# One GpSimd drain more behind the first scatter of the last pair of output tiles: sparse attention over a graph

## The chip, the cores and the metric

The kernel runs on one core of a Trainium2 chip. The metric is the device time of one execution in microseconds (us). The kernel before takes 637.19 us, the median of three runs (636.75 to 637.22).

The core's engines run side by side, each with its own stream of instructions: TensorE (PE; PEld are its weight loads), VectorE (DVE), ScalarE (ACT), GpSimd (POOL) and SyncE (SP). They wait for each other by semaphores. An engine's own sequencer takes its instructions in order; waits, branches and drains are the sequencer's work (in the profile POOLq, SPq and so on).

## The reference

A pre-norm layer with attention over a sparse graph: 2708 nodes of 1024 features, and a 0/1 matrix `adj` with a share of 0.0014771 ones, some four in a row.

```python
h = jnp.maximum(_layernorm(x, axis=-1), 0.0)
q = h @ W_q.T + b_q
k = h @ W_k.T + b_k
v = h @ W_v.T + b_v
z = scale * (q @ k.T)
spare_z = z * adj
spare_z = jnp.where(spare_z == 0.0, -10000.0, spare_z)
attn = jax.nn.softmax(spare_z, axis=1)
return x + jax.nn.relu(attn @ v)
```

## The kernel before

The kernel never forms the 2708 x 2708 scores. It finds each row's few neighbours in `adj`, and sorts the rows by their number of neighbours, so that the 21 full tiles of 128 sorted rows (and a rest of 20) each need about the same number of gathers. `ptab` holds, for each sorted place, the neighbours' row numbers and the row's own number (column `SLOTS`).

The stages, in order:

- M = W_q^T W_k is formed on TensorE from the weights as they come in; meanwhile rows of x are normed to h and stored to HBM, and VectorE searches `adj`.
- Ten "q" units: each takes two tiles of h and multiplies them with M. A unit is a two by two block product with seven multiplications instead of eight (`multiply`), two tiles of 128 rows against a 1024 x 1024 matrix.
- Beside them, for each tile, GpSimd gathers the neighbours' rows of h, VectorE takes their products with q, ScalarE the exponentials, and VectorE the weighted sum u of the gathered rows (`scores`, `weights`, `sums`).
- Ten "o" units: the same block product of two tiles of u with W_v. The tiles' order is fixed by the list `order`; its last entry is tile 8, which is left over and handled alone at the end.

An output tile is brought back to its place by an indirect DMA of GpSimd (`scatter`): the rows of y go to the rows of `out` whose numbers stand in `ptab`. All GpSimd DMAs, gathers and scatters, direct and indirect, go through one queue whose descriptors GpSimd makes itself.

The last o unit is the pair of tiles 16 and 9. For it `o_results` returns what `ends` returns: the rows of x are gathered ahead into ya (tile 16) and yb (tile 9), and as each bank of the product is done, VectorE adds the halves (`joined_x`: max with 0, plus x). `multiply` calls the four results in the order `c11` (left half of ya), `c12` (right half of ya), `c22` (right half of yb), `c21` (left half of yb). So tile 16 is complete in `c12`, which ends with its scatter, and tile 9 only in `c21`, after two more block products. Between them TensorE also starts the single tile 8.

Tile 8 follows with three block products; its right half is joined on VectorE and scattered (`scatter_half`), then the left half. Ahead of them, a flag is formed that tells whether the fast path held for this input; every engine reads it, and the branch behind it skips a general version of the kernel (lines 1390 on) that these inputs don't need. At the end (the profile gives it line 1562) SyncE waits for the landing of every DMA and for the other engines, and a barrier over all engines follows: each engine's sequencer drains and signals, GpSimd collects the signals and releases the others. These drains are put there by the framework; the kernel's own text has none.

The stream of GpSimd is not written out by hand at this point: a scheduler places instructions by their dependences, and `tc.issue_after(i)` places what is written under it behind instruction i on the same engine, without a wait for i to end.

Of the kernel before, what the change touches and what calls it, by code (L numbers as in the profile page):

```python
# [65 lines left out]
def tile_preln_masked_attention(  # L66
# [12 lines left out]
    nc = tc.nc  # L79
# [527 lines left out]
    def gather(dst, src, t, w, n, skip=False):  # L607
        off = bass.IndirectOffsetOnAxis(ap=ptab.bitcast(U32)[:n, t, w:w + 1], axis=0)
        if skip:
            return nc.gpsimd.indirect_dma_start(out=dst, out_offset=None, in_=src, in_offset=off,  # L610
                                                bounds_check=N - 1, oob_is_err=False)
        return nc.gpsimd.indirect_dma_start(out=dst, out_offset=None, in_=src, in_offset=off)
# [192 lines left out]
    outs = []  # L805

    def scatter(y, t, n):
        to = nc.gpsimd.indirect_dma_start(  # L808
            out=out, out_offset=bass.IndirectOffsetOnAxis(ap=ptab.bitcast(U32)[:n, t, SLOTS:SLOTS + 1], axis=0),
            in_=y[:n], in_offset=None)  # L810
        for other in outs:
            tc.declare_no_dep(to.ins, other.ins, reason="rows of a permutation")
        outs.append(to)
# [297 lines left out]
    def o_results(ta, tb):  # L1111
        ya = work.tile([P, D], FT, tag="q", name=f"y_{ta}", bufs=4)
        yb = work.tile([P, D], FT, tag="q", name=f"y_{tb}", bufs=4)
        if (ta, tb) == o_pairs[-1]:
            return ends(ya, ta, yb, tb)

        def c11(X):
            nc.scalar.activation(ya[:, lo], X, AF.Relu)

        def c22(Y, p5):  # L1120
            nc.vector.tensor_add(p5, copied(Y), p5)
            nc.scalar.activation(yb[:, hi], p5, AF.Relu)

        def c12(Z, u2):
            nc.vector.tensor_add(u2, Z, u2)
            nc.scalar.activation(ya[:, hi], u2, AF.Relu)  # L1126
            if ta == NT - 2:

                nc.sync.dma_start(tail_dram, ya[P - 1:, :])
            due.append((now[0], 5, ya, ta))  # L1130

        def c21(Y):
            nc.scalar.activation(yb[:, lo], Y, AF.Relu)
            due.append((now[0] + 1, 1, yb, tb))

        return c11, c22, c12, c21

    def ends(ya, ta, yb, tb):

        send(gather(ya, x, ta, SLOTS, P))  # L1140
        gather(yb, x, tb, SLOTS, P)

        def joined_x(y, cols, a):
            nc.vector.scalar_tensor_tensor(y[:, cols], a, 0.0, y[:, cols], op0=ALU.max, op1=ALU.add)

        def c11(X):
            joined_x(ya, lo, X)

        def c22(Y, p5):
            nc.vector.tensor_add(p5, Y, p5)  # L1150
            joined_x(yb, hi, p5)

        def c12(Z, u2):
            nc.vector.tensor_add(u2, Z, u2)
            joined_x(ya, hi, u2)
            scatter(ya, ta, P)

        def c21(Y):
            joined_x(yb, lo, Y)
            scatter(yb, tb, P)  # L1160

        return c11, c22, c12, c21
# [10 lines left out]
    def send(behind, stay=0):  # L1173

        while len(sent) > stay:
            with tc.issue_after(behind.ins):
                scatter(*sent.pop(0))
# [388 lines left out]
```

## Time and profile before

| what | value |
| --- | --- |
| median of three runs | 637.19 us (636.75 to 637.22) |
| span of the profiled execution, first to last instruction | 635.2 us |
| busy: TensorE, its weight loads | 624.2 us, 316.4 us |
| busy: VectorE, GpSimd, ScalarE | 523.9, 367.3, 285.9 us |
| GpSimd's DMA queue | 27,088 packets, 86.02 MB |
| mean granted clock of TensorE | 0.996 |
| issue to landing of the last pair's and the last tile's scatters (five from 600 us on) | 2.7 to 5.3 us |

The profile is of one execution; its span leaves out what lies before the first and after the last instruction, and so is some 2 us under the median. Busy time counts work alone: waits, branches and drains of a sequencer are not in it, and where they matter they have to be asked for by their line. In rows of the profile, "x3: 46/109/7122, 627.2 to 634.9" means three instructions with the shortest, median and longest duration in ns, and the start of the first and the last in us.

### The profile page before, as it was taken

The page shows a single profiled execution, that of the slowest core. Times are in us where ns is not written, and L with a number is a line of the kernel's source. Part 1 is how long each engine was busy: PE and PEld are TensorE (multiplying, and loading weights), DVE is VectorE, ACT ScalarE, POOL GpSimd, SP SyncE. Part 2 cuts the span into 40 slices and gives each one's busy share as a digit, 9 for nine tenths or more (in the row PEclk, how much of TensorE's full clock was granted, in tenths as well). Part 3 has the DMA queues.
Part 4 walks back from the last instruction along what each step waited for, and adds up shares of the span by engine and source line. Part 5 has one row for each costly group of instructions (what it writes and reads, how often), then busy time and mean ns, then how long its engine had stood idle before and what let it go on. Part 6 is the DMA issues. An engine that isn't in the chain of part 4 may idle for free.

```text
span 635.2 us, 6138 instructions
## 1 busy us (share of the span) xinstructions
PE 624.2 (98%) x1627; PEld 316.4 (50%) x1627; DVE 523.9 (82%) x1020; ACT 285.9 (45%) x423; POOL 367.3 (58%) x397
## 2 busy tenths in 40 slices
PE   9999999999999999999999999999999999999993
PEld 5777766444444544444444444444444444444441
DVE  5999888998896755997889999999899999898231
ACT  3538985749667553424341244343343342432200
POOL 2639960885877277564742644586678868622421
PEclk9999999999999999999999999999999999999998
DMA  8999997598796539996599997999999989993851
GB/s 340 407 369 310 342 356 288 203 325 310 261 360 237 182 118 323 342 351 220 188 295 365 307 399 227 322 346 294 386 354 289 336 276 284 278 269 80 242 189 37
DMA packets 62497, 181.16 MB, mean 285 GB/s; under 512 B 10055, under 2 KB 17047, under 8 KB 61688
## 3 DMA queue, kind: packets, MB, share of 16 engines
q0 software_dynamic: 27088, 86.02, 42.6%
q1 hardware_dynamic: 29434, 73.63, 33.2%
q10 hardware_dynamic: 5934, 21.06, 8.5%
q8 instruction: 15, 0.25, 0.1%
q14 instruction: 26, 0.21, 0.1%
HBM read 148.27 MB, written 42.31 MB: 300 GB/s over the span
## 4 chain that ended last, share of the span: by engine, by line
PE 98%; POOL 0%; DVE 0%; POOLq 0%; issue 0%
PE ps L1010 45%; PE psy L1010 32%; PE ps_y L476 6%; PE ps_z L476 4%; PE ps_x L476 4%; PE pt L415 4%; PE ps_y L511 1%; PE ps_h L1222 0%; PE ps_v L594 0%; DVE y_alone L1382 0%; POOL out_dram L1366 0%; POOLq L1388 0%; POOL hsum L121 0%; PE ps_all L680 0%; PE ps_in L678 0%
## 5 line engine op out<-in xcount | busy, mean ns | idle before, releaser
L610 POOL DMA_INDIRECT g<-h_dram,tab x94 | 119.6, 1272 | 62.1 <-ACT u L912 19.1
L1010 PE MATMUL ps<-M,a 128*128 128x512 f32 x320 | 144.0, 593 | 0.0
L1010 PE MATMUL psy<-wlow,s 128*128 128x512 f32 x320 | 143.9, 593 | 0.0
L863 DVE SCALAR_TENSOR_TENSOR junk<-g,pq 128x1024 uint8<-128x1024 f32 x93 | 113.7, 1223 | 12.8 <-DMA g<-h_dram,tab 8.9
L1010 PE MATMUL ps<-M,s 128*128 128x512 f32 x240 | 107.9, 593 | 0.0
L1010 PEld LDWEIGHTS ps<-M,a 128*128 128x128 f32 x320 | 59.9, 190 | 70.7 <-issue 70.0
L1010 PEld LDWEIGHTS psy<-wlow,s 128*128 128x128 f32 x320 | 59.8, 190 | 70.0 <-issue 69.1
L923 DVE SCALAR_TENSOR_TENSOR u<-g,coef,u 128x1024 f32<-128x1024 f32 x69 | 88.4, 1282 | 6.9 <-ACT u L912 5.8
L389 DVE FIND_INDEX8 at<-ones,adj 128x8 uint32<-128x685 f32 (+1 forms) x88 | 74.5, 864 | 0.0
L1010 PEld LDWEIGHTS ps<-M,s 128*128 128x128 f32 x240 | 45.6, 190 | 57.1 <-issue 55.9
L1010 PE MATMUL psy<-wlow,a 128*128 128x512 f32 x160 | 71.9, 593 | 0.0
L368 ACT ACTIVATE sized<-adj 128x2708 uint8<-128x2708 f32 (+1 forms) x22 | 54.3, 2467 | 7.3 <-DMA adj<-in_adj_dram 6.0
L298 POOL TENSOR_TENSOR hsum<-hsum,x 128x256 f32<-128x256 f32 (+1 forms) x56 | 38.6, 726 | 26.2 <-DVE wlow L444 21.6
L1109 POOL DMA_INDIRECT y<-in_x_dram,tab x19 | 32.7, 1723 | 30.5 <-ACT y L1126 15.7
L1010 PEld LDWEIGHTS psy<-wlow,a 128*128 128x128 f32 x160 | 30.5, 190 | 38.2 <-issue 37.5
L1010 PE MATMUL ps<-wlow,s 128*128 128x512 f32 x80 | 36.0, 592 | 0.0
L912 ACT ACTIVATE u<-g,coef 128x1024 f32<-128x1024 f32 x18 | 20.7, 1148 | 29.9 <-DVE coef L911 29.8
L808 POOL DMA_INDIRECT out_dram<-y,tab x21 | 25.3, 1206 | 15.2 <-DVE flag L1357 7.1
L626 POOL DMA_INDIRECT tab_dram<-tab,pos_i x22 | 21.9, 993 | 18.8 <-DVE pos_i L689 13.3
L276 ACT ACTIVATE x<-x,r 128x1024 f32<-128x1024 f32 (+1 forms) x22 | 25.9, 1233 | 7.2 <-POOL r L266 7.2
L944 ACT COPY v<-u 128x1024 f32<-128x1024 f32 x13 | 13.6, 1046 | 32.5 <-DVE u L923 28.2
L476 PE MATMUL ps_y<-wlow 128*128 128x512 f32 x64 | 27.6, 593 | 0.0
(252 smaller groups left out, 851.7 us busy)
## 6 DMA issues: line engine op xcount, KB each, us to landing
adj<-in_adj_dram SPq DMA_DIRECT2D x21, 1354.0 KB, 10.4
x<-in_x_dram SPq DMA_DIRECT2D x21, 512.0 KB, 11.0
h_dram<-x ACTq DMA_DIRECT2D x21, 512.0 KB, 7.3
u_dram<-v ACTq DMA_DIRECT2D x13, 512.0 KB, 6.6
or<-u_dram SPq DMA_DIRECT2D x52, 128.0 KB, 6.4
q_late<-q SPq DMA_DIRECT2D x12, 512.0 KB, 7.1
pq<-q_late POOLq DMA_DIRECT2D x12, 512.0 KB, 8.0
M<-in_wv_dram SPq DMA_DIRECT2D x4, 1024.0 KB, 10.4
```

Of the source, the lines that this page charges most:

```text
L276: nc.scalar.activation(xs[i][:n], xs[i][:n], AF.Relu, bias=r[:n, 4, i:i + 1], scale=r[:n, 3, i:i + 1])
L298: small.append(nc.gpsimd.tensor_add(hsum[:n, cols], hsum[:n, cols], xt[:n, cols]))
L368: nc.scalar.activation(sized[:n], a[:n, :, :PW], AF.Abs, accum_out=total[:n, t:t + 1])
L389: nc.vector.max_index(at[:n, k - first_k, g, :], ones[:n, 0:8], a[:n, g, :])
L415: nc.tensor.transpose(pt[:, c, :], xt[:, k * P:(k + 1) * P], ident)
L476: mm = nc.tensor.matmul(bank, a_tile(o + H * a[0], a[1], i), b(o), start=first and o == 0, stop=(o == H - 1), skip_group_check=True)
L610: return nc.gpsimd.indirect_dma_start(out=dst, out_offset=None, in_=src, in_offset=off, bounds_check=N - 1, oob_is_err=False)
L808: to = nc.gpsimd.indirect_dma_start(out=out, out_offset=bass.IndirectOffsetOnAxis(ap=ptab.bitcast(U32)[:n, t, SLOTS:SLOTS + 1], axis=0), i ...
L863: chained(lambda: nc.vector.scalar_tensor_tensor(junk, g_of[t][s], 1.0, tq[t], op0=ALU.mult, op1=ALU.mult, accum_out=zall[:, t, s:s + 1]))
L923: chained(lambda: nc.vector.scalar_tensor_tensor(u, g_of[t][s], coef[:, s:s + 1], u, op0=ALU.mult, op1=ALU.add))
L1010: mm = nc.tensor.matmul(bank, a[:, c, :], b[:, c, :], start=False, stop=(c == 3), skip_group_check=True)
L1109: return nc.gpsimd.indirect_dma_start(out=y[:n], out_offset=None, in_=x, in_offset=off, compute_op=ALU.add)
```

## The change

Behind the scatter of tile 16 (the first tile of the last pair) stands one more instruction on GpSimd: a drain, written so that it follows that scatter on GpSimd's stream.

```diff
@@ -1154,6 +1154,8 @@
             nc.vector.tensor_add(u2, Z, u2)
             joined_x(ya, hi, u2)
             scatter(ya, ta, P)
+            with tc.issue_after(outs[-1].ins):
+                nc.gpsimd.drain()
 
         def c21(Y):
             joined_x(yb, lo, Y)
```

`outs[-1]` is the scatter that was just issued. In the built program the drain stands directly behind it, and directly ahead of the waits and the scatter of tile 9; it waits for no semaphore and signals none. No other instruction of any engine changes its place, and no wait is added or taken away elsewhere. The lines of the file behind this place move down by two: what is line 1366 or 1562 before is 1368 or 1564 after.

## The prediction

> **What bounds the kernel now.** I began with the page, to see whether TensorE or something else sets the time, and then left it for the end of the program, because that is where the added instruction stands.
>
> ```profile
> span 635.2 us, 6138 instructions
> PE 624.2 (98%) x1627; PEld 316.4 (50%) x1627; DVE 523.9 (82%) x1020; ACT 285.9 (45%) x423; POOL 367.3 (58%) x397
> q0 software_dynamic: 27088, 86.02, 42.6%
> ```
>
> TensorE is busy for 624.2 of 635.2 us. So some 11 us of the span hold no matmul, and a GpSimd instruction can be paid for or can save only there, or where it makes a matmul late. The last row is GpSimd's own DMA queue: 27,088 packets in the whole run. The chain of waits shows where the last matmul lies and what follows it.
>
> ```profile
> 615.00 10.42 PE ps L1010 x24
> 625.45 0.70 DVE y_alone L1382
> 626.18 0.50 POOLq L1388
> 626.68 0.69 POOL out_dram L1366
> ```
>
> The columns are start, length, and engine with line. TensorE ends at 625.4, VectorE joins the last half tile, GpSimd issues the last scatter of the output, and there the chain stops at 627.4. The span runs on to 635.2, so 7.8 us at the end belong to nothing that counts as work. I asked for line 1562, the end of the program, first from 627 to 634 us and then from 634 on:
>
> ```profile
> L1562 SPq EVENT_SEMAPHORE  x12: 27/28/28, 629.7 to 630.4; - x12
> L1562 SPq DRAIN  x2: 7/10/13, 630.4 to 630.5; - x2
> L1562 POOLq DRAIN  x1: 7122/7122/7122, 627.2 to 627.2; - x1
> L1562 DVEq DRAIN  x1: 17/17/17, 629.2 to 629.2; - x1
> ...
> L1562 POOLq EVENT_SEMAPHORE  x4: 17/17/17, 634.4 to 635.1; - x4
> L1562 POOLq DRAIN  x3: 46/109/7122, 627.2 to 634.9; - x3
> ```
>
> The numbers after "x" are the shortest, median and longest duration in ns, then the first and last start. GpSimd's sequencer (POOLq) runs one drain of 7.122 us, from 627.2 to 634.4, and its next instruction, the first step of the barrier that ends the program, starts at 634.4. SyncE has been through its own list of twelve waits, the landing of the last scatter among them, by 630.5. The waits of SyncE say how long it then stood:
>
> ```profile
> SPq L1562 <- DMA out_dram<-y_alone,half_i: 10.3, 1, 10.3
> SPq L1562 <- PEq L1562: 4.6, 2, 4.1
> ```
>
> It stood 4.1 us at the barrier (the longest of two waits there; the row puts it down to TensorE's sequencer, which takes part in the same barrier). What ended last is therefore GpSimd's drain, by 634.4 - 630.5 = 3.9 us over the next thing.
>
> **What the drain does in these 7.1 us.** It does not only wait for data. The last scatter and its landing:
>
> ```profile
> L1366 POOL DMA_INDIRECT out_dram<-y_alone,half_i x1: 963/963/963, 626.4 to 626.4; - x1
> DMA to landing us min/median/max: 3.2/3.2/3.2
> ```
>
> It landed at 626.4 + 3.2 = 629.6, and the drain went on for another 4.8 us. Nor is this the price of any drain of GpSimd: of the three drains at the end the other two took 109 and 46 ns, with no DMA between them and the long one, and the one at the program's start, ahead of every DMA, took 184 ns:
>
> ```profile
> L1555 POOLq DRAIN  x1: 184/184/184, 0.4 to 0.4; - x1
> ```
>
> So the long drain works something off that DMAs leave behind, and the one right after it finds nothing left. The trace has one drain behind DMAs and so cannot tell whether the price grows with what was issued since the last drain (or is owed once), or is the same after a single DMA. This is the point on which the forecast turns.
>
> **The change, part by part.** One drain is added to GpSimd's stream; it has no semaphore of its own, no DMA is added, and on the other four engines nothing moves. It stands between two scatters, both of which are rows here:
>
> ```profile
> 607.86 0.96 POOL L808 DMA_INDIRECT out_dram<-y,tab  x1 [0.77 <-DVE many L1354]
> 615.89 0.95 POOL L808 DMA_INDIRECT out_dram<-y,tab  x1 [7.06 <-DVE flag L1357]
> 623.77 0.97 POOL L1366 DMA_INDIRECT out_dram<-y_alone,half_i  x1 [6.93 <-DVE y_alone L1379]
> 626.41 0.96 POOL L1366 DMA_INDIRECT out_dram<-y_alone,half_i  x1 [1.67 <-DVE y_alone L1382]
> ```
>
> These are tiles 16 and 9 of the last pair and the two halves of the last single tile. GpSimd idles 7.06 us ahead of the second, since tile 9 is joined on VectorE only then:
>
> ```profile
> 614.92 0.69 DVE L1144 SCALAR_TENSOR_TENSOR y<-psy,y 128x512 f32<-128x512 f32 x1 [4.98 <-PE psy L1010]
> ```
>
> *The added drain.* In the trace the long drain started 0.8 us after the start of the DMA ahead of it (627.2 against 626.41), so this one starts between 607.9 and 608.8. Its length is not in the trace. From below it is the 0.11 us of a drain with nothing to do. From above it first waits for tile 16's rows and then works for the whole 7.12 us; the five scatters from 600 us on landed within 2.7 to 5.3 us of issue:
>
> ```profile
> L808 POOL DMA_INDIRECT out_dram<-y,tab x3: 952/965/982, 606.1 to 615.9; - x3
> L1366 POOL DMA_INDIRECT out_dram<-y_alone,half_i x2: 963/965/967, 623.8 to 626.4; - x2
> ...
> DMA to landing us min/median/max: 2.7/3.5/5.3
> ```
>
> That is at most 607.86 + 5.3 + 7.1 = 620.3. I take 7.1 us from 608.3, an end at 615.4: all but three of the program's GpSimd DMAs stand ahead of it, so if it works them off it has what the last drain has now. Behind it on GpSimd wait tile 9's scatter and the two halves, and for these only the end of the program waits. Two DMAs of GpSimd follow each other at 0.97 + 0.30 us, so tile 9's scatter may start as late as 623.77 - 1.27 = 622.5 before a half is late. Every value up to the upper bound lies ahead of that: the cost on the path is 0, hidden in GpSimd's 7.06 us and, past those, in the 6.93 us ahead of the next scatter. Without either cover it would be its whole length, 7.1 us.
>
> *The last drain.* It now has three scatters behind it instead of the whole run's DMAs. From below it must last until the last landing, 629.6, or 2.4 us; from above 7.12 us as now. I take the lower end and 0.1 us more, an end at 629.7, because the two short drains show that what one drain has done the next does not do again.
>
> *What is late next.* SyncE's list, at 630.5. It needs the same landing and goes through its waits one after another, and the change does not touch it. The barrier's first step moves from 634.4 to 630.5, and the 0.8 us from there to 635.2 stays. Sum: 0 + (630.5 - 634.4) = -3.9 us; the span goes from 635.2 to 631.3. The median of the runs is 637.19, 2.0 us over this execution's span, for what lies around it; that stays: 637.2 - 3.9 = **633.3 us**.
>
> The Trainium skill, "VectorE: DVE Perf Modes", section "The DRAIN you can't avoid", speaks against this: drains of the preamble and postamble are a constant of about 12 ns on all five engines. By that rule neither drain has a length worth moving and the sum would be 0, 637.2 us. The trace agrees for SyncE and VectorE (7 to 17 ns) and not for GpSimd, whose drain took 7122 ns.
>
> **The rivals.** *The price is fixed.* Any drain that has a GpSimd DMA ahead of it needs some 4.8 us after the last landing, however few there were (some check of the rings from end to end). Then the added drain costs as much, hidden, and the last one stays at 7.1 us: **637.2 us**. For it: the trace has a single long drain. Against it: 4.8 us is long beside the 0.96 us in which GpSimd makes a whole scatter, and 27,088 packets are much to leave behind. That the added drain does nothing at all comes to the same time.
>
> The Trainium skill, "PSUM — Partial Sum Buffer", section "Engine vs sequencer instructions", says that a drain waits for the engine to go fully idle, and knows no backlog; taken alone that is this rival. The trace shows the engine's last work ending at 627.4 and the drain only at 634.4, so idleness in that sense is not what it waited for.
>
> *Part and part.* Some of the price is fixed: with half of the 4.8 us left the last drain ends at 629.6 + 2.4 = 632.0, still over SyncE's 630.5, and the gain is 634.4 - 632.0 = 2.4 us: **634.8 us**.
>
> *The queue is held, and it is slower.* The added drain holds GpSimd's stream, with three output scatters behind it. It decides from 622.5 us on, a length of some 14 us, twice the long drain. At three times the long drain, 21.4 us, it would end at 608.3 + 21.4 = 629.7, the last scatter would start two slots of 1.27 us later at 632.2 instead of 626.4, and all behind it would be 5.8 us late: SyncE's list at 636.3, against 634.4 for the end of the drain now, even with a short last drain: 637.2 + 1.9 = **639.1 us**, and 637.2 + 5.8 = 643.0 with a long one. For it: the row of 5.3 us is the slowest landing of this stretch, so transfers do collect just there. Against it: 12.4 us, landing and full length one after the other, is the most that the rows give.
>
> **How the numbers follow.** The full gain 0.72, part and part 0.06, fixed 0.17, held 0.05. I lean to the first because the 109 ns drain shows a debt that is paid off, and because every bound on the hidden side leaves room. Its own range is 632.7 to 634.2: the runs before lie 0.5 us apart, and the last drain may end up to 0.7 us behind SyncE's list. With part and part it holds 0.78, so the range has to reach to the unchanged time: 632.7 to 637.2. A change of under 0.2% (1.3 us) is what a measurement here cannot tell from none; faster by more are the first two, 0.78, within it the third, 0.17, slower the last, 0.05.
>
> **What would show it.** Right: a drain on line 1158 of about 7 us from about 608 us on; tile 9's scatter within 1 us of 615.9; the long drain at the end 2 to 3 us instead of 7.1; SyncE's longest wait at the barrier close to 0 instead of 4.1; the same last matmul at 625.4. Wrong at the step on the last drain: it still takes 7 us while the added one took anything at all. Wrong at the step on the cover: the scatters after the added drain start late and the last landing moves.

## The result, and the profile after

| | before | with the drain |
| --- | --- | --- |
| median | 637.15 us (636.75 to 637.22, 4 runs) | 633.1 us (632.89 to 633.31, 4 runs) |
| ratio | | 0.9938, 95% interval 0.9924 to 0.9952 |
| span of the profiled execution | 635.2 us | 631.1 us |

The forecast was 633.3 us. Line 1562 of before, the end of the program, is line 1564 now; the added drain is line 1158. Both by their lines (count, shortest/median/longest duration in ns, first and last start in us):

```profile
L1158 POOLq DRAIN  x1: 10251/10251/10251, 607.2 to 607.2; - x1
```

```profile
L1564 POOLq EVENT_SEMAPHORE  x4: 17/17/17, 630.3 to 631.0; - x4
L1564 POOLq DRAIN  x3: 46/109/2374, 627.2 to 630.8; - x3
L1564 SPq DRAIN  x3: 7/7/13, 630.2 to 630.5; - x3
```

The drain at the end starts where it did, at 627.2, and takes 2.374 us instead of 7.122. It ends at 629.6, and the barrier begins at 630.3 behind SyncE's list instead of at 634.4 behind the drain. The waits of SyncE (total, times, longest) show the same from the other side: where it stood 4.1 us at the barrier, 0.5 is left.

```profile
SPq L1564 <- DMA out_dram<-y_alone,half_i: 10.0, 1, 10.0
...
SPq L1564 <- PEq L1564: 0.7, 2, 0.5
```

What the added drain holds is in the timeline of GpSimd (start, length, idle time before it and its cause):

```profile
608.29 0.97 POOL L808 DMA_INDIRECT out_dram<-y,tab  x1 [0.30 <-issue]
618.22 0.95 POOL L808 DMA_INDIRECT out_dram<-y,tab  x1 [8.97 <-issue]
623.75 0.96 POOL L1368 DMA_INDIRECT out_dram<-y_alone,half_i  x1 [4.58 <-DVE y_alone L1381]
626.39 0.96 POOL L1368 DMA_INDIRECT out_dram<-y_alone,half_i  x1 [1.68 <-DVE y_alone L1384]
```

Tile 9's scatter starts at 618.22 instead of 615.89, and "issue" in place of VectorE says that it no longer waited for another engine (VectorE had joined tile 9 by 615.6): the drain, from 607.2 to 617.4, held it. The scatter behind it waits for VectorE again, and starts 0.02 us from its old place. The lateness is used up in the idle time before it. The chain of waits ends as before, with the last matmul at the same time:

```profile
614.98 10.42 PE ps L1010 x24
625.40 0.02 issue
625.42 0.70 DVE y_alone L1384
```

### The profile page after: what moved, and what is told of

It reads as the page before. It is cut to its first block, busy times and chain, and to the rows that moved or that the text cites. A ratio compares the mean times of both kernels' runs of the same rounds, so it can differ in the third digit from the quotient of the medians.

```text
span 631.1 us, 6139 instructions
## 1 busy us (share of the span) xinstructions
PE 624.2 (99%) x1627; PEld 315.8 (50%) x1627; DVE 524.0 (83%) x1020; ACT 286.6 (45%) x423; POOL 368.2 (58%) x397
## 4 chain that ended last, share of the span: by engine, by line
PE 99%; POOL 0%; DVE 0%; POOLq 0%; issue 0%
PE ps L1010 46%; PE psy L1010 33%; PE ps_y L476 7%; PE ps_z L476 4%; PE ps_x L476 4%; PE pt L415 4%; PE ps_y L511 1%; PE ps_h L1224 0%; PE ps_v L594 0%; DVE y_alone L1384 0%; POOL out_dram L1368 0%; POOLq L1390 0%; POOL hsum L121 0%; PE ps_all L680 0%; PE ps_in L678 0%
## 5 line engine op out<-in xcount | busy, mean ns | idle before, releaser
L1109 POOL DMA_INDIRECT y<-in_x_dram,tab x19 | 34.3, 1807 | 31.3 <-ACT y L1126 15.7
L760 ACT COPY ps<-bp_sb 128x512 f32<-128x512 f32 x42 | 24.6, 596 | 6.1 <-DVE y L1144 5.5
```

The source lines that it names most:

```text
L1109: return nc.gpsimd.indirect_dma_start(out=y[:n], out_offset=None, in_=x, in_offset=off, compute_op=ALU.add)
```

## The experiments

Three questions: does the cover matter, does the place matter, and what is it that the drain works off? For the third I read one figure from each trace, the end of a drain less the last landing of the GpSimd DMAs ahead of it, and call it the drain's **rest**. (A landing is read from the semaphore events of GpSimd's own DMAs; those of the other engines' DMAs don't count.) In the profile before, the rest is 634.36 - 629.65 = 4.71 us for 213 DMAs; with the change it is 4.59 us for 210 at the added drain and 0.17 us for 3 at the end.

The runs were made in three groups. The first (both runs on the cover, the early drain's first run, the first ladder) ran where the kernel before took 639.7 us, the second (the 15th scatter, the ladder on gathers) where it took 640.1, the third (the repeats) where it took 637.1. So times are compared as ratios to before in the same group, and starts within one run only.

**The cover, used up.** The drain behind tile 9's scatter instead of tile 16's:

```diff
             joined_x(yb, lo, Y)
             scatter(yb, tb, P)
+            with tc.issue_after(outs[-1].ins):
+                nc.gpsimd.drain()
```

> The drain behind tile 9's scatter instead of tile 16's. Tile 9's scatter is back at 615.9 and lands near 619.4; the drain works 4.7 us after it, to 624.1; the first half's scatter starts at 624.4 instead of 623.8, the last half's at 626.4 as before. Theory of the cover: nothing of it is exposed, time 633.1 us like the change. If the two halves need more room than one slot of 1.27 us, the last scatter is late by what lies over it and the time is up to 634 us.

Ratio 0.9926 (0.9907 to 0.9945), as for the change. GpSimd in this run:

```profile
619.00 0.95 POOL L808 DMA_INDIRECT out_dram<-y,tab  x1 [7.03 <-DVE flag L1359]
627.95 0.96 POOL L1368 DMA_INDIRECT out_dram<-y_alone,half_i  x1 [8.00 <-issue]
629.52 0.97 POOL L1368 DMA_INDIRECT out_dram<-y_alone,half_i  x1 [0.61 <-DVE y_alone L1384]
```

Tile 9's scatter is not held any more; the first half tile is (8.00 us of "issue"), and the last one still waits for VectorE, for 0.61 us. So the cover reaches this far with 0.6 us to spare.

**The cover, gone.** The drain between the two half scatters of the last tile:

```diff
     scatter_half(1, hi)
+    with tc.issue_after(outs[-1].ins):
+        nc.gpsimd.drain()
     add_block(X, uT[:, 4:8, :], M[:, 1, 0])
```

> The drain between the two half scatters of the last tile, where nothing covers it. The first half lands near 626.5, the drain works 4.7 us to 631.2, the last half's scatter starts near 631.5 instead of 626.4 and lands near 634.5; SyncE's list ends near 635.3. Time 633.1 + 5.1 = 638.2 us, slower than before by 1.0 us, though the last drain is as short as in the change. If the drain doesn't hold the DMA behind it, 633 us.

Ratio 1.0024 (1.0012 to 1.0036): slower than before, by about 640 x 0.0024 = 1.5 us. The two halves and the drain between them:

```profile
626.58 0.96 POOL L1366 DMA_INDIRECT out_dram<-y_alone,half_i  x1 [6.93 <-DVE y_alone L1379]
634.69 0.96 POOL L1366 DMA_INDIRECT out_dram<-y_alone,half_i  x1 [7.15 <-issue]
```

```profile
L1382 POOLq DRAIN  x1: 7617/7617/7617, 626.3 to 626.3; - x1
```

The drain at the end is short here too, 2.579 us, yet the last scatter starts 634.69 - 626.58 = 8.1 us after the first, where before it was 2.64. The 5.5 us by which it is late outweigh what the end saves. Forecast was 5.1 us.

**Another covered place.** One drain behind the 15th scatter, where GpSimd then waits 12 us (the counter stands in `scatter`):

```diff
         outs.append(to)
+        if len(outs) == 15:
+            with tc.issue_after(to.ins):
+                nc.gpsimd.drain()
```

> One drain, behind scatter 15 near 573 us, where GpSimd then stands idle for 12 us instead of 7. 200 DMAs ahead of it, 13 behind. It waits for its landings and works some 4.2 us, ends near 584 and holds nothing. The drain at the end has 13 DMAs: at the 41 ns a DMA of the ladder's short steps it works 0.6 us after the last landing, under the 0.85 us that SyncE's list takes, so it stays covered. Time as the change, a ratio of 0.994 to before; tile 9's scatter back within 0.1 us of its place. If only the tail of the program is a good place, a ratio nearer 1.

Ratio 0.9948 (0.9927 to 0.9968). The added drain took 11.677 us with a rest of 4.18 for 200 DMAs; the one at the end 2.986 us with a rest of 0.58 for 13 DMAs, under SyncE's list, as forecast. So the gain is not tied to the program's last pair of tiles: this other covered place serves as well.

**What is worked off.** First the extreme: the same counter with `len(outs) == 1`, one early drain at 117 of the 213 DMAs.

> The added drain moved from tile 16's scatter to the first scatter of the program, near 415 us, with 117 of the 213 GpSimd DMAs ahead of it and 96 behind. Theory A (a debt per DMA: 4.7 us of work for 213 DMAs, 22 ns each, since the drain before): the early drain works 117 x 22 ns = 2.6 us after its last landing, the one at the end 96 x 22 ns = 2.1 us after its last landing at 629.4, so it ends near 631.6 instead of 634.4; time about 634.4 us, plus what the held gathers cost, which shows as a later last matmul. Theory B (owed once, by the first drain that finds DMAs behind it): the early drain works some 4.7 us, the one at the end 0.2 us, time about 633.1 us plus the same holding cost.

Ratio 1.0019 (0.9997 to 1.004). Both theories are wrong. The early drain has a rest of 0.79 us only, and the one at the end one of 5.70, more than in the kernel before, for less than half its DMAs. To see whether this repeats, I ran it once more, and the kernel before with it:

> The early drain once more, profiled anew: steps of 117 and 96 DMAs, which left 0.8 and 5.7 us. If that belongs to the program, the same again. If to the execution: other values, of which 4.8 and 4.0 us (41 ns a DMA) are the likeliest single ones when nothing is dropped.

> The kernel before once more, profiled anew, to see whether the debt belongs to the program or to the execution. If to the program: the drain at the end again works 4.7 us after its last landing, for 213 DMAs, where 41 ns each would make 8.7. If to the execution (GpSimd drops done entries at a place that differs from run to run): anything from 0.1 to 8.7 us, and not 4.7.

The end of the early drain's second run, line 1565 there:

```profile
L1565 POOLq DRAIN  x3: 46/109/8043, 628.5 to 637.2; - x3
L1565 SPq DRAIN  x3: 7/7/13, 631.5 to 636.9; - x3
```

8.043 us at the end, against 8.042 in the first profile, and 0.79 us of rest at the early drain again; the kernel before has 4.71 us again (in a drain of 6.890 us, since its last landing came 0.2 us sooner). The rest of the end drain is 5.84 us this time, with the same length, since its landing came 0.13 us sooner after its start. So these figures look to belong to the program and not to the execution. In this pair, one run each, the early drain costs 639.14 - 636.71 = 2.4 us: the drain at the end ends 636.59 - 634.15 = 2.4 us later. Of these 1.1 us are the longer drain's (8.04 against 6.89), and 1.3 us are the last matmul's, which ends at 626.7 instead of 625.4. Of the latter, 0.4 us arose ahead of the early drain and don't come from it (by 412.5 us TensorE had stood idle for 1.57 us instead of 1.18); 0.85 us are a wait of TensorE for VectorE at 612 us. That this wait goes back to the gathers held behind the early drain (the first starts at 425.4 instead of 416.4) is likely and not shown.

Then the ladder, with the counter at 1, 3, 8, 14 and 15 on top of the change:

> The change with five more drains, behind scatters 1, 3, 8, 14 and 15, so that seven drains have 117, 12, 27, 42, 2, 10 and 3 DMAs between them. Read from each: its end less the last landing of the DMAs ahead of it. Theory A: 2.6, 0.3, 0.6, 0.9, 0.05, 0.2 and 0.1 us, a line through about 0.1 us with 22 ns a DMA. Theory B: 4.7 us at the first, 0.2 us or less at each of the others. Theory C (a fixed price as soon as one DMA is ahead): falls if any of them is under 1 us. The time itself is not compared, since the drains hold gathers.

Seven drains of one run, by line: the five of the counter, the change's, and the end's.

```profile
L816 POOLq DRAIN  x5: 7377/12095/13343, 416.2 to 592.6; - x5
```

```profile
L1161 POOLq DRAIN  x1: 6410/6410/6410, 627.5 to 627.5; - x1
```

```profile
L1567 POOLq DRAIN  x3: 51/109/2434, 643.2 to 646.9; - x3
```

Their lengths say little, because most of each is the wait for landings; their rests say more. For 117, 12, 27, 42, 2, 10 and 3 DMAs they are 0.79, 0.54, 1.15, 1.76, 0.12, 0.45 and 0.16 us. But for the first, this is a line: 0.05 us and 0.041 us for each DMA since the last drain, twice the 22 ns that I had from 4.71 us over 213. Theory C falls as well, at 0.12 us for two DMAs. Three runs more, with a counter on the gathers of h rows, were to find where the long stretches leave it:

```diff
                     gathered.append(gather(g, h_dram[:, :], t, s, P, skip=True))
+                if len(gathered) in (6, 54, 76):
+                    with tc.issue_after(gathered[-1].ins):
+                        nc.gpsimd.drain()
```

> Drains behind three gathers, so that four drains have 40, 70, 39 and 64 DMAs since the one before. Read: the end of each less the last landing ahead of it. Theory D (41 ns a DMA since the last drain, as in the ladder's steps of 1 to 42): 1.7, 2.9, 1.6 and 2.7 us. Theory E (GpSimd also drops done entries by itself while it goes on issuing, so that a long stretch leaves less than its count): the steps of 40 and 39 on the line, those of 70 and 64 under it. Theory F (a long stretch adds something, as the 5.7 us for 96 did): 64 and 70 above it.

The second of them has (22, 84) there, the third (40,).

> Two drains behind other gathers, for steps of 67, 97 and 49 DMAs. Theory D: 2.8, 4.0 and 2.0 us. Theory E: less than that at 97. Theory F: about 5.7 us at 97, as for the 96 of the early drain.

> One drain behind the 90th DMA, for steps of 90 and 123. Theory D: 3.7 and 5.1 us. Theory E: the first 90 leave less than that (117 left 0.8 us, 210 left 4.6), and 123 too. Theory F: 5.4 us or more at 123.

All rests, by the number of DMAs since the last drain; "line" is 0.05 + 0.041 for each:

| DMAs since the last drain | rest, us | line, us |
| --- | --- | --- |
| 1, 2, 3, 10, 12, 13 | 0.09, 0.13, 0.17, 0.45, 0.54, 0.58 | 0.09, 0.13, 0.17, 0.46, 0.54, 0.58 |
| 27, 39, 40, 42, 49 | 1.15, 1.63, 1.69, 1.76, 2.05 | 1.16, 1.65, 1.69, 1.77, 2.06 |
| 67, 70, 90, 97 | 2.79, 2.90, 3.73, 4.01 | 2.80, 2.92, 3.74, 4.03 |
| 64, 96 | 3.14, 5.70 (5.84 when run again) | 2.67, 3.99 |
| 117, 123 | 0.79, 0.66 | 4.85, 5.09 |
| 200, 210, 211, 212, 213 | 4.18, 4.59, 4.63, 4.67, 4.71 | 8.25, 8.66, 8.70, 8.74, 8.78 |

Up to 97 DMAs all points but two lie on the line, which is theory D; E and F, as they were stated, fail at 70, 90 and 97. The last row is parallel to the line, 41 ns from each count to the next, but 4.07 us lower, and 117 is lower by the same 4.06 us: some hundred DMAs are no longer in the debt. That is theory E for the longest stretches. These six stretches begin with the program, and so do those of 40, 67 and 90, which lose nothing; so what is lost goes between the 90th and the 117th DMA. 123, a stretch that begins behind the 90th, is lower by 4.43 us.

64 and 96 lie above the line, as theory F would have it, but longer stretches don't. These two are drains at the end, whose landing came 2.2 to 2.3 us after their start; their whole lengths, 5.43 and 8.04 us, are 84 to 85 ns for each DMA, twice the line's slope, as if the debt were gone through once beside the wait for the landing and once after it. That the length stayed at 8.04 us when the landing came 0.13 us sooner speaks for it. Against it stand the drains with 211 to 213 DMAs: their landings came 2.2 to 3.8 us after their start, too soon for a first pass of 4.7 us beside the wait, and yet they show one rest of 4.6 to 4.7 us and no second. So why 64 and 96 leave more is open.

The third of these runs has its only added drain at 352 us, and 123 DMAs after it, but the drain at its end (line 1565 there) is nearly as short as the change's:

```profile
L1565 POOLq DRAIN  x3: 46/109/2856, 629.7 to 633.3; - x3
L1565 SPq DRAIN  x3: 7/7/13, 632.6 to 633.0; - x3
```

It took 635.33 us, one run, where before took 640.11 (638.28 to 641.8 in 11 runs), a ratio of 0.9925. An early drain can thus gain as much as the change (here) or cost time (behind the first scatter). The rest that it leaves to the end is 0.66 us here and 5.7 there; what decides between the two is not shown.

**The change once more**, beside the repeats:

> The change once more, on the chip of the other experiments and with more runs. Its ratio to before as on record, 0.994, and its last drain 0.2 us behind the last landing whatever the drain on line 1158 found: with 3 DMAs there is nothing to drop. The spread of its times is narrower than that of before, if before's last drain differs from execution to execution.

Ratio 0.9943 (0.993 to 0.9957), with rests of 4.59 and 0.17 us again. The spread, 633.1 to 634.12, is not clearly narrower than that of before, 636.87 to 638.15.

## Why the prediction was right

**What bounds the end: right.** That GpSimd's drain, and no matmul, DMA or list of waits, ended last by 3.9 us was read from rows of line 1562, and the change, which touched only that, moved the end by 635.2 - 631.1 = 4.1 us. This agreement is the test; the stated range reached to the unchanged time, and that the result lies in it says little.

**The last drain: right.** Forecast 2.5 us with an end at 629.7; measured 2.374 us with an end at 629.6. The step rested on the two short drains, that what one drain has done the next does not do again. Every later run with so few DMAs bears it out: drains with 1 to 3 of them since the last drain have rests of 0.09 to 0.17 us. The rival of a fixed price falls with that, and so does "part and part", which left 2.4 us. The step is not good for any place, though: 96 DMAs behind an early drain left 5.7 us.

**What is late next: right.** SyncE's list, forecast to end at 630.5, ended at 630.3; the landing came 3.0 us after the issue where the row of before had 3.2.

**The added drain: right in its place and its cover, mis-sized in its length.** "An end at 615.4", 7.1 us from 608.3; measured 10.251 us, from 607.2 to 617.4. Two terms were off. The drain began 1.1 us before the scatter that it stands behind had begun on GpSimd (608.29); its sequencer was ahead of the engine. And I had taken the length of the last drain over as a whole, though that is a wait for the landing and a rest: the rest was nearly the same (4.59 against 4.71 us), but the scatter ahead landed at 612.84, 4.6 us after its issue, instead of 3.2:

```profile
L808 POOL DMA_INDIRECT out_dram<-y,tab x1: 967/967/967, 608.3 to 608.3; - x1
DMA to landing us min/median/max: 4.6/4.6/4.6
```

The sum should have been landing and rest, 608.3 + 4.6 + 4.6 = 617.5. The upper bound, 620.3, was made in that way and held. So "tile 9's scatter within 1 us of 615.9" was wrong by 1.3 us, at no cost, as the part on the cover had it: a half is late only from 622.5 on. The run with the drain between the halves shows the price when that point is passed, with the mechanism of the rival in which the queue is held, at another place.

**What the price is: left open in the forecast, half settled now.** "Grows with what was issued since the last drain (or is owed once)": it is not owed once, since 97 DMAs behind an earlier drain left 4.01 us and 12 left 0.54. It grows at 41 ns a DMA on stretches of up to 97, but for two that left more, and stretches of 117 and more lose 4.1 to 4.4 us of it by something that these runs don't show. That the forecast came out does not depend on it: the drain stood three DMAs ahead of the end.

The Trainium skill, "GPSIMD Engine Reference", section "2.1 Instruction dispatch", has another way to owe something once: the first call of freshly loaded code costs some 6 us that no instruction of the profile shows. The rests do not agree with that as the cause here, since they follow the count of DMAs and come again at the second and third drain of a run.

**Open:** by what GpSimd drops a part of the debt, and why two end drains took longer. The drop repeats exactly (0.79 us in three profiles, 4.71 in two), so it hangs on the program's own course, and from the program's start it lies between the 90th and the 117th DMA. Whether it is a count, a place in the queue or an instruction that does it wasn't tried.

## What to carry to other kernels

A kernel that issues many DMAs from GpSimd can, like this one, owe its end several us that no busy time, no DMA and no chain of waits shows; ask for the last line's drains, and compare GpSimd's with the last landing and with SyncE's list. If it ends last, a drain put where GpSimd idles anyway, a few DMAs ahead of the end, takes that off the path; it needs idle time for the landing ahead of it plus the rest, and a place with only short work behind it. The gain stops at the next thing that waits for the last landing.

## What was not expected of the hardware

A drain begins before the DMA that it stands behind has started on GpSimd (607.18 against 608.29 us, and 608.43 against 608.67 when run again). An added drain early in the program made the drain at its end longer, 8.04 us against 6.9 to 7.1, although fewer DMAs were left for it. And the rest of a drain fits a line of 41 ns a DMA within 0.02 us over fifteen counts from 1 to 97, all that were measured but 64 and 96, and it follows the count and not the packets: a step of 42 had 5,984 packets, one of 40 only 2,752, with rests of 1.76 and 1.69 us.
